# Layer 1 of a convolution–attention kernel: normalising in the channel layout with means and factors spread through DRAM, weight sums issued one by one, bias split moved

## The chip, the cores and the metric

The kernel runs on one core of a Trainium2 chip. A core has TensorE (matrix products), VectorE, ScalarE, GpSimd and SyncE, each with its own in-order queue; SyncE's queue issues the DMAs here. The metric is the device time of one launch in microseconds (us). Before the change it is 3277.91 us, the median of three runs (3275.79 to 3279.31).

## The reference, cut to what matters

The input is 8 images of 256 channels by 32x32 positions. Layer 0 (convolutions and attention) is not touched. Layer 1 takes each image as t, 1024 tokens of 256 channels:

```
def _ln_t(v, eps=1e-5):
    m = jnp.mean(v, axis=-1, keepdims=True)
    s = jnp.var(v, axis=-1, keepdims=True)
    return (v - m) / jnp.sqrt(s + eps)

t = t + _L1_attn_ref(_ln_t(t), WQ, WK, WV)        # causal attention, one head of 256
t = t + _L1_ffn_ref(_ln_t(t), Wr, br, W1, ...)    # 8 experts, three products each, gated by a softmax
```

The gate uses the mean of the second norm over the 8 images; each expert's last product adds a bias bo, weighted by the gate.

## The kernel before, in words

Layer 0 comes first, then layer 1's attention image by image, then the experts. All of t lies with channels on the 128 rows (two groups, KC = 2) and tokens along the row; the mean over channels is therefore a sum across rows.

`layer_norm` (L1351) does a norm in token layout. For each pair of 128-token tiles TensorE transposes t into PSUM (tile tpt, four transposes), ScalarE copies that to zt, and VectorE takes mean and variance of each token (`bn_stats`, `bn_aggr`, into mv). GpSimd makes the factor r from the variance in six small steps. Then VectorE scales zt in place (`scaled`, one 128x256 operation per tile), TensorE transposes it back (tile tpz, four transposes a pair), and ScalarE copies the result to the destination. It is used for the first norm (z of image b+1), for the second norm (z2 of image b-1, written to z_d), and in a half form for the last image (`second_norm_half`, L1440).

`causal(b)` (L1458) is the main stream of attention of image b: per 128-token tile i the scores s (TensorE, `scores`), their maximum nm (VectorE), the exponential (ScalarE), `norm` (masking, sum and reciprocal on VectorE, scaling on GpSimd), two to three tiles later `turn` (transposes tp, copies pT), and per 256 tokens `product` (po), which is added to t. The last quarter of image b-1 is done while image b runs.

`beside(b)` (L1532) is the side stream: first norm of b+1, a wait (`until`) for the last product of b-1, second norm of b-1, then `keys_values(b + 1)` (products pk and pv; the scores of b+1 need kk, z). `together` (L411) weaves both by hand: each generator yields its estimated us, and the side may run while its sum is under 0.85 times the main's. What is left of the side is issued after the main stream of that image is over. The engines keep this order. DMAs are placed by the scheduler into SyncE's queue.

There are three buffers for t. After the second norm of b, `second_norm` writes z_d and u_d (z2 and t) and loads t of b+3 into the freed buffer (L1432 to L1434). GpSimd adds z2 to feat. From image 2 on `weight_sums` (L1248) advances by one expert matrix per score tile: four VectorE operations of 128x128 at once and a DMA to sums_d.

At the start of the experts, from L1586: boT is made from the bias bo (split into two parts of low precision, transposed), in a pool hp that reuses the attention's memory; then `fetch(0)`, `fetch(1)`, the loads of the last half norm, and the 18 loads of sums_d are queued. Expert 0's first product pa needs none of them, expert 1's needs its sums ws.

Of the kernel before, what the change touches and what calls it, by code (L numbers as in the profile page):

```python
# [9 lines left out]
F32 = mybir.dt.float32  # L10
# [63 lines left out]
def conv_attn_hybrid_kernel(  # L74
# [1173 lines left out]
    def weight_sums(space):  # L1248


        for e in range(NE):
            for l in (0, 1, 2) if seven(e) else (0, 2):
                w_ = w_of[e][l]
                if e == 0:
                    s_ = sums_of[e][l] = wm.tile([P, 3, P], F32, tag=f"ws{e}_{l}", name=f"ws{e}_{l}")
                else:
                    s_ = space.tile([P, 3, P], F32, tag="ws", name="ws", bufs=2)
                a11, a21, a12, a22 = (w_[:, k, g * P : (g + 1) * P] for k in range(KC) for g in range(KC))
                dve.tensor_add(s_[:, 0, :], a21, a22)
                dve.tensor_sub(s_[:, 1, :], s_[:, 0, :], a11)  # L1260
                dve.tensor_sub(a21, a11, a21)
                dve.tensor_sub(s_[:, 2, :], a12, s_[:, 1, :])
                if e:
                    nc.sync.dma_start(sums_d[e, l], s_)
                yield
# [47 lines left out]
    with ExitStack() as l1:  # L1313
# [37 lines left out]
        def layer_norm(b, dst, tiles=range(NT)):  # L1351


            t0, n = tiles[0], len(tiles)
            zt = two.tile([P, NT, C], F32, tag="zt", name="zt", bufs=1)
            mv = tiny.tile([P, NT, 2], F32, tag="mv", name="mv", bufs=2)
            for i0 in range(0, n, 2):
                tp = ps_t.tile([P, 2, C], F32, tag="tp", name="tpt")
                for i in range(2):
                    for k in range(KC):  # L1360
                        c0 = (t0 + i0 + i) * P
                        pe.transpose(tp[:, i, k * P : (k + 1) * P], t[b][:, k, c0 : c0 + P], ident)
# [17 lines left out]
            for _ in range(4):  # L1380
# [6 lines left out]
            scaled(0)  # L1387
            yield 0.5
            for i0 in range(0, n, 2):
                if i0 + 2 < n:  # L1390
                    scaled(i0 + 2)
# [5 lines left out]
                yield 0.9  # L1397

        def first_norm(b):
            z[b] = two.tile([P, KC, N], F32, tag="z", name="z1")  # L1400
            yield from layer_norm(b, z[b])

        def keys_values(b):
            kk = kk_of[b] = two.tile([P, KC, N], F32, tag="kk", name="kk")
            for h in range(2):
                hs = slice(h * HALF, (h + 1) * HALF)
                for g in range(KC):
                    pk = ps_m.tile([P, HALF], F32, tag="mm", name="pk")
                    for k in range(KC):
                        pe.matmul(pk, at[:, k, g * P : (g + 1) * P], z[b][:, k, hs], start=(k == 0), stop=(k == KC - 1))  # L1410
                    act.copy(kk[:, g, hs], pk)
                    yield 1.7
            v = v_of[b] = two.tile([P, NT, C], F32, tag="v", name="v")
# [10 lines left out]
            while what not in done:  # L1424
                yield 0.7

        def second_norm(b):
            yield from until((b, N // QC - 1))
            z2 = two.tile([P, KC, N], F32, tag="z2", name="z2", bufs=1)
            yield from layer_norm(b, z2)  # L1430
            nc.sync.dma_start(z_d[b], z2)
            nc.sync.dma_start(u_d[b], t[b])  # L1432
            if b + 3 < B:
                load_t(b + 3)  # L1434
            if b == 0:
                pool.tensor_copy(feat, z2)
            else:
                pool.tensor_add(feat, feat, z2)
# [19 lines left out]
        def causal(b):  # L1458
            for i in range(NT):
                yield from scores(b, i)  # L1460
                yield from follow()
                if b >= 2:
                    next(sums, None)

        def follow():
# [10 lines left out]
        def scores(b, i):  # L1476
            q0, width = i * P, (i + 1) * P
            s = ps_s.tile([P, N], F32, tag="s", name="s1")
            for h in range(2):
                hs = slice(h * HALF, (h + 1) * HALF)  # L1480
                for k in range(KC):
                    pe.matmul(s[:, hs], z[b][:, k, q0:width], kk_of[b][:, k, hs], start=(k == 0), stop=(k == KC - 1))
                yield 1.7

            nm = tiny.tile([P, 1], F32, tag="nm", name="nm1")
# [44 lines left out]
            done.add((b, qc))  # L1530

        def beside(b):  # L1532
            if b + 1 < B:
                yield from first_norm(b + 1)
            if b >= 1:
                yield from second_norm(b - 1)
            if b + 1 < B:
                yield from keys_values(b + 1)
            else:
                yield from second_norm_half(b)  # L1540
                yield from gate(
                    0, feat, ps_m.tile([P, NT // 2, NE], F32, tag="mm", name="lg"), lambda: ps_t.tile([4 * NE, HALF], F32, tag="tp", name="pwT")
                )
# [8 lines left out]
        sums = weight_sums(two)  # L1552
        for _ in first_norm(0):
            pass
        for _ in keys_values(0):
            pass
        load_t(2)
        for b in range(B):

            if b == 2:  # L1560
                z0 = wm.tile([P, KC, HALF], F32, name="z0")
                nc.sync.dma_start(z0, z_d[0][:, :, :HALF])
            if b == 4:
                tz0 = column_sums(z0, wm.tile([P, 4, QC], F32, tag="tz0", name="tz0"))
            together(last() if b == B - 1 else causal(b), beside(b), 0.85)
        nc.sync.dma_start(u_d[B - 1][:, :, HALF:], t[B - 1][:, :, HALF:])
# [14 lines left out]
    with ExitStack() as l2:  # L1581
# [10 lines left out]
        bo_g = cols("bo").rearrange("p (e g) -> p g e", g=KC).unsqueeze(2).to_broadcast([P, KC, 2, NE])  # L1592
        bo4 = hp.tile([P, KC, 4, NE], F32R, name="bo4", bufs=1)
        dve.tensor_copy(bo4[:, :, 0:2, :], bo_g)
        dve.tensor_sub(bo4[:, :, 2:4, :], bo_g, bo4[:, :, 0:2, :].bitcast(F32))
        pb = ps_b.tile([4 * NE, KC, P], F32, tag="pm", name="pbo")
        for g in range(KC):
            pe.transpose(pb[:, g, :], bo4[:, g].bitcast(F32).rearrange("p a e -> p (a e)"), ident)
        dve.tensor_copy(boT, pb)
# [206 lines left out]
        zs[halves[0]] = z0  # L1806
        fetch(0)
        fetch(1)
        between = last_norm()
        next(between)  # L1810
        tz[halves[0]] = tz0
        for e in range(1, NE):
            for l in (0, 1, 2) if seven(e) else (0, 2):
                sums_of[e][l] = hp.tile([P, 3, P], F32, tag=f"ws{e}_{l}", name=f"ws{e}_{l}", bufs=1)
                nc.sync.dma_start(sums_of[e][l], sums_d[e, l])
        LAG2, LAG3 = 2, 4
        for n in range(len(pieces) + LAG3):
            one_ = two_ = three = iter(())
# [144 lines left out]
```

## Time and profile before

One execution was profiled; it took 3277.43 us, of which 3275.3 us are the span from its first to its last instruction.

| What | Before |
|---|---|
| median of the runs | 3277.91 us |
| profiled execution, and its span | 3277.43 us, 3275.3 us |
| TensorE busy | 3047.3 us, 93% |
| VectorE busy | 2417.4 us, 74% |
| ScalarE busy | 1438.2 us, 44% |
| GpSimd busy | 327.9 us, 10% |
| attention of layer 1, first scores to first expert product | 1439.63 to 2041.49 us |
| image 0 / 1 / 2 / 3 | 56.2 / 75.4 / 77.6 / 77.4 us |
| image 4 / 5 / 6 / 7 | 75.8 / 76.1 / 74.4 / 89.0 us |

Times inside the profile are us from the start of the span. A row of a timeline is: start, duration, engine, line, operation, output<-input, matrix or tile shape, count, and in brackets the idle time before it with what ended it. A matrix product of 32-bit numbers appears as two TensorE records. Nearly all rows carry L68, the line of the helper that keeps the program's order, so rows are told apart by tile names. The duration of a merged TensorE row includes the tail of its last product; the distance between starts is what TensorE is taken up.

### The profile page before, as it was taken

The numbers are of one execution on the slowest core, as the hardware profiler recorded it, in microseconds if no ns is written. First come the engines' busy times: TensorE is split into PE (matmuls) and PEld (weight loads), VectorE is DVE, ScalarE is ACT, GpSimd is POOL, SyncE is SP. The second block draws the span as 40 slices with busy tenths as digits, with TensorE's granted clock in tenths as the row PEclk, the third lists the DMA queues.
The fourth block names the chain that finished last, engine by engine and source line by source line (L and its number), as shares of the span: only waits on it lengthen the run. The fifth ranks groups of instructions, "written<-read, shape, count | busy, mean of one in ns | idle before, by whom it ended". The sixth has DMA issues, their size and how long they took to land.

```text
span 3275.3 us, 43158 instructions
## 1 busy us (share of the span) xinstructions
PE 3047.3 (93%) x17218; PEld 2050.7 (63%) x17218; DVE 2417.4 (74%) x3796; ACT 1438.2 (44%) x2227; POOL 327.9 (10%) x472
## 2 busy tenths in 40 slices
PE   7997999999999997779999998899999999999999
PEld 4554555555555554346556665678787777787787
DVE  5388888888888886735555444688888878888887
ACT  4554555555555553223333322444444444444443
POOL 2110212111111100011222111000000000000000
PEclk9998999999999999889999999999999999999999
DMA  3202020202020200031111101200000100000000
GB/s 111 53 1 52 27 52 27 53 27 52 27 52 27 52 14 20 4 136 44 50 61 51 39 26 72 75 20 20 20 20 20 33 20 20 20 20 26 20 7 13
DMA packets 49831, 121.45 MB, mean 37 GB/s; under 512 B 7302, under 2 KB 20054, under 8 KB 45782
## 3 DMA queue, kind: packets, MB, share of 16 engines
q1 hardware_dynamic: 49622, 118.61, 11.6%
q8 instruction: 137, 2.24, 0.3%
q14 instruction: 72, 0.59, 0.1%
HBM read 48.20 MB, written 37.88 MB: 26 GB/s over the span
## 4 chain that ended last, share of the span: by engine, by line
PE 48%; DVE 6%; ACT 1%; issue 1%; POOL 1%; DMA 0%; SPq 0%; ACTq 0%; POOLq 0%; DVEq 0%
PE pm L68 13%; PE pa L68 12%; PE q L68 12%; PE s L68 4%; PE po L68 3%; PE pv L68 2%; PE pk L68 2%; DVE nm L68 1%; DVE pr L68 1%; DVE zt L68 1%; DVE st L68 1%; ACT pr L68 1%; PE tp L68 1%; PE tpz L68 1%; PE tpt L68 1%
## 5 line engine op out<-in xcount | busy, mean ns | idle before, releaser
L68 ACT ACTIVATE h<-h,bn_o,bn_s 128x512 f32<-128x512 f32 x384 | 308.7, 813 | 627.7 <-DVE h L68 627.6
L68 DVE SCALAR_TENSOR_TENSOR x<-hpad,vec,x 128x1024 f32<-128x1024 f32 x248 | 320.4, 1297 | 32.1 <-ACT x L68 25.9
L68 DVE SCALAR_TENSOR_TENSOR conv<-hpad,vec,conv 128x1024 f32<-128x1024 f32 x256 | 331.5, 1301 | 14.3 <-ACT conv L68 8.4
L68 PE MATMUL pm<-h,w 128*128 128x512 f32 (+1 forms) x768 | 321.5, 528 | 0.0
L68 ACT ACTIVATE pT<-s 128x1024 f32<-128x1024 f32 x256 | 261.5, 1024 | 128.1 <-PE s L68 127.0
L68 PE MATMUL po<-pT,vT 128*32 128x256 f32 x4096 | 276.7, 388 | 12.0 <-ACT pT L68 11.3
L68 PE MATMUL ph<-xn,piw 128*128 128x512 f32 x512 | 250.8, 615 | 22.7 <-ACT conv L68 14.2
L68 PE MATMUL s<-kk,z 128*128 128x512 f32 x512 | 242.0, 600 | 0.6 <-DVE pr L68 0.6
L68 PE MATMUL s<-qst,kst 128*128 128x256 f32 x1024 | 216.5, 334 | 0.0
L68 PEld LDWEIGHTS s<-qst,kst 128*128 128x128 f32 x1024 | 146.5, 191 | 88.5 <-issue 82.2
L68 PEld LDWEIGHTS pm<-h,w 128*128 128x128 f32 x768 | 146.9, 191 | 76.6 <-issue 62.6
L68 DVE TENSOR_TENSOR h<-pa,first 128x512 f32<-128x512 f32 x128 | 88.3, 689 | 136.0 <-PE pa L68 134.3
L68 ACT ACTIVATE hpad<-ph,pi_o 128x512 f32<-128x512 f32 x126 | 87.0, 690 | 228.5 <-PE ph L68 228.4
L68 DVE TENSOR_TENSOR h<-h,wb 128x1024 f32<-128x1024 f32 x128 | 156.2, 1221 | 41.0 <-ACT h L68 41.0
L68 DVE SCALAR_TENSOR_TENSOR o<-vpad,pe_w,o 128x1024 f32<-128x1024 f32 x128 | 163.6, 1283 | 17.4 <-ACT o L68 14.7
L68 DVE TENSOR_TENSOR h<-h,first 128x256 f32<-128x256 f32 x384 | 163.2, 425 | 13.2
L68 PEld LDWEIGHTS ph<-xn,piw 128*128 128x128 f32 x512 | 88.9, 190 | 132.1 <-issue 89.1
L68 PE MATMUL pz<-pow__117,hid 128*128 128x256 f32 x512 | 129.2, 408 | 44.4 <-DVE hid L68 44.4
L68 PEld LDWEIGHTS po<-pT,vT 128*32 128x32 f32 x4096 | 107.5, 109 | 97.1 <-ACT pT L68 15.2
L68 PE MATMUL sums<-pT,ones 128*32 128x256 f32 x2048 | 158.7, 382 | 0.0
L68 PE MATMUL pa<-tz,ws 128*128 128x256 f32 x512 | 155.0, 385 | 3.8 <-DMA ws<-sums_d 3.8
L68 PE MATMUL q<-t,ws 128*128 128x256 f32 x512 | 152.8, 380 | 0.8 <-DVE t L68 0.8
(279 smaller groups left out, 5870.6 us busy)
## 6 DMA issues: line engine op xcount, KB each, us to landing
td<-t SPq DMA_DIRECT2D x8, 1024.0 KB, 3.8
t<-td SPq DMA_DIRECT2D x8, 1024.0 KB, 4.8
te<-ud SPq DMA_DIRECT2D x16, 512.0 KB, 4.0
out_dram<-te SPq DMA_DIRECT2D x16, 512.0 KB, 2.8
ze<-zd SPq DMA_DIRECT2D x15, 512.0 KB, 3.9
t<-in_x_dram SPq DMA_DIRECT2D x7, 1024.0 KB, 6.3
qst<-hi SPq DMA_DIRECT2D x56, 128.0 KB, 2.3
qst<-lo SPq DMA_DIRECT2D x56, 128.0 KB, 2.3
```

The costliest lines, as they stand in the source:

```text
L68: return self._tc.keep_in_program_order(method(*args, **kwargs))
```

## The change

The first norm of images 1 to 7 and the second norm of images 0 to 6 no longer go through zt and back. `statistics` transposes t and takes mean and variance as before (with the destination as scratch), GpSimd makes r and copies the means beside it, TensorE transposes this 128x16 tile (tpr), ScalarE copies it (rmT), and a DMA writes 16 rows of 128 numbers, 8 KB, to DRAM. `to_all_rows` reads them back with one DMA into rb, the same 8 KB on each of the 128 rows (1 MB, in the one buffer that zt has). `apply` computes (t - mean) * factor in t's own layout, eight VectorE operations of 128x512. `first_norm(0)` and the half norm keep `layer_norm`, whose pauses and look-ahead are changed.

The side stream is reordered: statistics(b+1), the wait, statistics(b-1), apply(b+1), keys, apply(b-1) with its DMAs, values. The load of t of b+3 stays in the step after the second norm, now `normed`, and so follows apply. Weight sums yield after every VectorE operation, start at image 1 and advance twice a tile. boT is made at the start of image 4. The queue at the start of the experts begins with the sums of expert 1.

```diff
+        def statistics(b, dst):
+            zt = dst.rearrange("p k n -> p (k n)").rearrange("p (i c) -> p i c", c=C)
...
+            pool.tensor_mul(r, r, y)
+            pool.tensor_copy(rm[:, 1, :], mv[:, :, 0])
+            for _ in range(4):
+                yield 1.0
+            tp = ps_t.tile([2 * NT, P], F32, tag="tp", name="tpr")
+            pe.transpose(tp, rm.rearrange("p a i -> p (a i)"), ident)
+            rmT = tiny.tile([2 * NT, P], F32, tag="rmT", name="rmT", bufs=1)
+            act.copy(rmT, tp)
+            rm_d[b] = dram.tile([2 * NT, P], F32, tag=f"rm{len(rm_d)}", name="rm_d")
+            nc.sync.dma_start(rm_d[b], rmT)
+            yield 0.2
+        def to_all_rows(b):
+            rb = rb_of[b] = two.tile([P, 2, N], F32, tag="zt", name="rb", bufs=1)
+            nc.sync.dma_start(rb.rearrange("p a n -> p (a n)"), rm_d.pop(b).rearrange("a n -> (a n)").partition_broadcast(P))
+        def apply(b, dst):
+            rb = rb_of.pop(b)
+            for h in range(2):
+                hs = slice(h * HALF, (h + 1) * HALF)
+                for k in range(KC):
+                    dve.tensor_sub(dst[:, k, hs], t[b][:, k, hs], rb[:, 1, hs])
+                    yield 0.6
+                    dve.tensor_mul(dst[:, k, hs], dst[:, k, hs], rb[:, 0, hs])
+                    yield 0.6
...
-        def second_norm(b):
-            yield from until((b, N // QC - 1))
-            z2 = two.tile([P, KC, N], F32, tag="z2", name="z2", bufs=1)
-            yield from layer_norm(b, z2)
+        def normed(b, z2):
             nc.sync.dma_start(z_d[b], z2)
             nc.sync.dma_start(u_d[b], t[b])
             if b + 3 < B:
...
         def beside(b):
-            if b + 1 < B:
-                yield from first_norm(b + 1)
+            more = b + 1 < B
+            if more:
+                z[b + 1] = two.tile([P, KC, N], F32, tag="z", name="z1")
+                yield from statistics(b + 1, z[b + 1])
+                to_all_rows(b + 1)
             if b >= 1:
-                yield from second_norm(b - 1)
-            if b + 1 < B:
-                yield from keys_values(b + 1)
+                yield from until((b - 1, N // QC - 1))
+                z2 = two.tile([P, KC, N], F32, tag="z2", name="z2", bufs=1)
+                yield from statistics(b - 1, z2)
+            else:
+                yield from pause(8)
+            if more:
+                yield from apply(b + 1, z[b + 1])
+            if b >= 1:
+                to_all_rows(b - 1)
+            if more:
+                yield from keys(b + 1)
+            else:
+                yield from pause(8)
+            if b >= 1:
+                yield from apply(b - 1, z2)
+                normed(b - 1, z2)
+            if more:
+                yield from values(b + 1)
             else:
                 yield from second_norm_half(b)
...
-        boT = hp.tile([4 * NE, KC, P], F32R, name="boT", bufs=1)
...
+                boT = wm.tile([4 * NE, KC, P], F32R, name="boT")
...
         zs[halves[0]] = z0
-        fetch(0)
-        fetch(1)
+        fetch_sums(1)
         between = last_norm()
         next(between)
+        fetch_sums(2)
+        fetch(0)
+        for e in range(3, NE):
+            fetch_sums(e)
+        fetch(1)
         tz[halves[0]] = tz0
```

More of the change, by code (lines that the diff above doesn't have):

```diff
@@ L1259, in weight_sums @@
                 dve.tensor_add(s_[:, 0, :], a21, a22)
+                yield
                 dve.tensor_sub(s_[:, 1, :], s_[:, 0, :], a11)
+                yield
                 dve.tensor_sub(a21, a11, a21)
+                yield
                 dve.tensor_sub(s_[:, 2, :], a12, s_[:, 1, :])
@@ L1378, in layer_norm @@
             pool.tensor_mul(r, r, y)
-            for _ in range(4):
+            for _ in range(6):
                 yield 1.0
@@ L1387, in layer_norm @@
             scaled(0)
+            if n > 2:
+                scaled(2)
             yield 0.5
             for i0 in range(0, n, 2):
-                if i0 + 2 < n:
-                    scaled(i0 + 2)
+                if i0 + 4 < n:
+                    scaled(i0 + 4)
                 tp = ps_t.tile([P, KC, 2, P], F32, tag="tp", name="tpz")
@@ L1397, in layer_norm @@
                 yield 0.9
+        rm_d, rb_of = {}, {}
+        def statistics(b, dst):
+            zt = dst.rearrange("p k n -> p (k n)").rearrange("p (i c) -> p i c", c=C)
+            mv = tiny.tile([P, NT, 2], F32, tag="mv", name="mv", bufs=2)
+            for i0 in range(0, NT, 2):
+                tp = ps_t.tile([P, 2, C], F32, tag="tp", name="tpt")
+                for i in range(2):
+                    for k in range(KC):
+                        c0 = (i0 + i) * P
+                        pe.transpose(tp[:, i, k * P : (k + 1) * P], t[b][:, k, c0 : c0 + P], ident)
+                act.copy(zt[:, i0 : i0 + 2, :], tp)
+                yield 0.6
+                for i in range(i0, i0 + 2):
+                    st = tiny.tile([P, 6], F32, tag="st", name="st")
+                    dve.bn_stats(st, zt[:, i, :])
+                    dve.bn_aggr(mv[:, i, :], st)
+                yield 0.6
+            y = tiny.tile([P, NT], F32, tag="y1", name="y1", bufs=2)
+            rm = tiny.tile([P, 2, NT], F32, tag="rm", name="rm", bufs=2)
+            r = rm[:, 0, :]
+            pool.tensor_scalar(y, mv[:, :, 1], LN_EPS, None, ALU.add)
+            pool.tensor_tensor(r, y, mhalf1, ALU.pow)
+            pool.tensor_mul(y, y, r)
+            pool.tensor_mul(y, y, r)
+            pool.tensor_scalar(y, y, -0.5, 1.5, ALU.mult, ALU.add)
+            pool.tensor_mul(r, r, y)
[9 more added lines that the diff above has]
+            yield 0.2
@@ new lines, in to_all_rows @@
+        def to_all_rows(b):
[5 more added lines that the diff above has]
+                hs = slice(h * HALF, (h + 1) * HALF)
+                for k in range(KC):
+                    dve.tensor_sub(dst[:, k, hs], t[b][:, k, hs], rb[:, 1, hs])
+                    yield 0.6
+                    dve.tensor_mul(dst[:, k, hs], dst[:, k, hs], rb[:, 0, hs])
+                    yield 0.6
@@ L1399, in first_norm, with pause @@
+        def pause(n):
+            for _ in range(n):
+                yield 1.0
         def first_norm(b):
@@ L1401, in first_norm, with keys @@
             yield from layer_norm(b, z[b])
-        def keys_values(b):
+        def keys(b):
             kk = kk_of[b] = two.tile([P, KC, N], F32, tag="kk", name="kk")
@@ L1412, in keys_values, with values @@
                     yield 1.7
+        def values(b):
             v = v_of[b] = two.tile([P, NT, C], F32, tag="v", name="v")
@@ L1461, in causal @@
                 yield from follow()
-                if b >= 2:
+                if b >= 1:
                     next(sums, None)
@@ L1482, in scores @@
                     pe.matmul(s[:, hs], z[b][:, k, q0:width], kk_of[b][:, k, hs], start=(k == 0), stop=(k == KC - 1))
+                if h == 0 and b >= 1:
+                    next(sums, None)
                 yield 1.7
@@ L1532, in beside @@
         def beside(b):
-            if b + 1 < B:
-                yield from first_norm(b + 1)
-            if b >= 1:
-                yield from second_norm(b - 1)
-            if b + 1 < B:
-                yield from keys_values(b + 1)
+            more = b + 1 < B
[3 more added lines that the diff above has]
+                to_all_rows(b + 1)
+            if b >= 1:
+                yield from until((b - 1, N // QC - 1))
[11 more added lines that the diff above has]
+                yield from pause(8)
+            if b >= 1:
+                yield from apply(b - 1, z2)
+                normed(b - 1, z2)
+            if more:
+                yield from values(b + 1)
             else:
@@ L1554, in conv_attn_hybrid_kernel @@
             pass
-        for _ in keys_values(0):
-            pass
+        for steps in (keys(0), values(0)):
+            for _ in steps:
+                pass
         load_t(2)
@@ L1563, in conv_attn_hybrid_kernel @@
             if b == 4:
+                boT = wm.tile([4 * NE, KC, P], F32R, name="boT")
+                bo_g = cols("bo").rearrange("p (e g) -> p g e", g=KC).unsqueeze(2).to_broadcast([P, KC, 2, NE])
+                bo4 = wm.tile([P, KC, 4, NE], F32R, name="bo4")
+                dve.tensor_copy(bo4[:, :, 0:2, :], bo_g)
+                dve.tensor_sub(bo4[:, :, 2:4, :], bo_g, bo4[:, :, 0:2, :].bitcast(F32))
+                pb = ps_m.tile([4 * NE, KC, P], F32, tag="mm", name="pbo")
+                for g in range(KC):
+                    pe.transpose(pb[:, g, :], bo4[:, g].bitcast(F32).rearrange("p a e -> p (a e)"), ident)
+                dve.tensor_copy(boT, pb)
                 tz0 = column_sums(z0, wm.tile([P, 4, QC], F32, tag="tz0", name="tz0"))
@@ L1587, in conv_attn_hybrid_kernel @@
         s2, o2 = bn_fold("g2", "be2", "m2", "v2", eps_moe, "bn2", extra="b2")
-        boT = hp.tile([4 * NE, KC, P], F32R, name="boT", bufs=1)
[L1592 to L1599, printed above, removed]
         def sums_tile(name):
@@ L1804, in last_norm, with fetch_sums @@
             )
-        zs[halves[0]] = z0
-        fetch(0)
-        fetch(1)
[L1809 to L1812, printed above, removed]
+        def fetch_sums(e):
             for l in (0, 1, 2) if seven(e) else (0, 2):
@@ L1815, in conv_attn_hybrid_kernel @@
                 nc.sync.dma_start(sums_of[e][l], sums_d[e, l])
+        zs[halves[0]] = z0
+        fetch_sums(1)
+        between = last_norm()
+        next(between)
+        fetch_sums(2)
[3 more added lines that the diff above has]
+        fetch(1)
+        tz[halves[0]] = tz0
         LAG2, LAG3 = 2, 4
```

## The prediction, on record before the run

> **What bounds the kernel now.** I read the page's busy times first, then a table of busy time by image, then the TensorE timeline of image 4 (an undisturbed one), with VectorE, GpSimd and the DMA queue beside it, and last the handover to the experts. The page says that TensorE sets the time:
>
> ```profile
> PE 3047.3 (93%) x17218; PEld 2050.7 (63%) x17218; DVE 2417.4 (74%) x3796; ACT 1438.2 (44%) x2227; POOL 327.9 (10%) x472
> ```
>
> So the change is worth what it takes off TensorE's own queue in the attention stage. By image (stretch: length, TensorE, weight loads, VectorE, ScalarE, GpSimd, clock, DMA):
>
> ```profile
> 1726.26:1802.05 75.79, 69.83 (x294) 45.44 (x293) 42.45 (x119) 24.20 (x44) 16.30 (x21) 1.00 0.14 55
> 1952.52:2041.49 88.97, 76.46 (x329) 53.84 (x329) 39.74 (x101) 20.15 (x38) 15.31 (x21) 0.94 0.12 48
> ```
>
> TensorE is idle 6 us of image 4. The groups of the stretch 1548 to 2000 show where:
>
> ```profile
> L68 PE MATMUL tpz<-ident,zt 128*128 128x128 f32 x176 | 30.9, 295 | 29.6 <-DVE zt L68 28.2 <-ACT z L68 1.4
> ```
>
> Nearly all idle time stands ahead of the transposes back (tpz), which the change removes. The TensorE timeline of image 4:
>
> ```profile
> 1716.98 1.88 PE L68 MATMUL s<-kk,z 128*128 128x512 f32 x4
> 1718.69 1.89 PE L68 MATMUL pv<-wv,z 128*128 128x256 f32 x8
> 1721.07 5.35 PE L68 MATMUL pv<-wv,z 128*128 128x256 f32 x24
> 1726.26 1.88 PE L68 MATMUL s<-kk,z 128*128 128x512 f32 x4
> 1727.97 1.04 PE L68 MATMUL tpt<-ident,t 128*128 128x128 f32 x8
> ...
> 1736.97 1.88 PE L68 MATMUL s<-kk,z 128*128 128x512 f32 x4
> 1739.92 0.67 PE L68 MATMUL tpz<-ident,zt 128*128 128x128 f32 x4 [1.07 <-DVE zt L68]
> ...
> 1766.11 3.60 PE L68 MATMUL s<-kk,z 128*128 128x512 f32 x8
> 1771.38 0.41 PE L68 MATMUL tpz<-ident,zt 128*128 128x128 f32 x2 [1.67 <-DVE zt L68]
> ...
> 1777.62 0.41 PE L68 MATMUL tpz<-ident,zt 128*128 128x128 f32 x2 [1.54 <-DVE zt L68]
> ```
>
> The reader is to see the period (scores of the image's last tile, values pv, next image's first scores at 1726.26, its transposes tpt at 1727.97) and the stalls. Beside it VectorE, GpSimd and the DMA queue:
>
> ```profile
> 1718.89 1.22 DVE L68 TENSOR_REDUCE nm<-s 128x1 f32<-128x1024 f32 x1 [3.36 <-PE s L68]
> 1724.04 0.17 DVE L68 RECIPROCAL rs<-rs 128x1 f32<-128x1 f32 x1
> 1725.88 0.68 DVE L68 TENSOR_TENSOR tz<-z 128x512 f32<-128x512 f32 x1
> 1739.07 0.20 POOL L68 TENSOR_TENSOR r<-r,y 128x8 f32<-128x8 f32 x1
> 1762.95 0.32 SPq L1324 DMA_DIRECT2D t<-td  x1
> ```
>
> The load of t is issued at 1762.95, right after the second norm's last tpt, and is needed at the next image's tpt near 1804: 41 us of slack for a transfer that lands in
>
> ```profile
> t<-td SPq DMA_DIRECT2D x8, 1024.0 KB, 4.8
> ```
>
> **What the Trainium skill says.** "TensorE: Matmul & The Clock Gate", What's actually happening: after an idle window of 3413 ns the array runs at half clock, until a busy window. The trace agrees: eight transposes take 1.94 us after 3.15 us of idleness, against 1.04 above.
>
> ```profile
> 1617.68 1.94 PE L68 MATMUL tpz<-ident,zt 128*128 128x128 f32 x8 [3.15 <-DVE zt L68]
> ```
>
> "SBUF — State Buffer", Who interferes with whom: a VectorE operation with two SBUF inputs contends with a GpSimd operation that reads SBUF. The trace agrees: w<-w takes 1.12 us at 1724.64 beside GpSimd's scaling, 0.29 at 1660.88 without. All eight operations of apply are of this kind. "DMA: Bandwidth & Descriptors", Rules for kernel authors: all 16 engines serve a DMA whose outermost dimension is a multiple of 16; the spread of rb has 128. No run here shows such a spread, and no page prices 128 reads of one row.
>
> **Part by part.** I cut image 4's period at Q = 1727.97 (tpt), E = 1755.52 (end of the last quarter's product) and T = 1794.49 (end of the last scores): Q to E 27.55, E to T 38.97, T to the next Q 9.3 us.
>
> Removed: 32 transposes at 0.11 us (eight take 0.87 start to start) are 3.5 us. Around them start-to-start gaps lose 1.2, 0.4, 0.8 (first norm) and 1.8, 0.5, 0.5, 1.7, 0.6 (second), 7.5 in all. Together 11 us an image.
>
> Added, by the order of the changed kernel's instructions on each engine:
>
> First tpr, between the two halves of tile 1's scores. GpSimd's r ends at 1739.27, 11.3 after Q; its copy of the means adds 0.25 (the y rows of the same shape). TensorE is there 10.7 after Q. Wait 0.9, transpose 0.2. Q to E becomes 27.55 - 4.3 + 1.1 = 24.35.
>
> Second tpr, inside tile 5's scores. Three of its four tpt groups now stand after tile 3's first half. VectorE does two groups of statistics (1.06 each), tile 3's maximum and norm (5.4 with ScalarE between), two weight sums, two groups; the last ends 12.7 after E, the GpSimd chain (3.43) at 16.3. TensorE is there at 12.8: wait 3.6. Behind it in TensorE's queue is everything else, tile 5's second half first.
>
> apply(b+1): eight operations at 0.68 (tz<-z row; 0.66 between starts). The first pk waits for the fourth of them, behind tile 5's maximum, norm and sums: ready 25.2 after E, TensorE there at 23.7, wait 1.5. The second pk waits for the addition of po to t, now behind the other four and tile 6's maximum: 1.2. E to T becomes 37.1.
>
> apply(b-1) and the load. After T, ScalarE's exponential waits for the last keys' copy (T+2.45), the norm ends at T+5.5, eight operations follow; the seventh, the last to read t, ends at T+10.9 (0.5 in it for GpSimd's scaling). Only then may t of b+2 be loaded into that buffer: 4.8 us, so Q comes at T+15.8. TensorE, after pk 1.7, turn 0.7, pv 6.9 and first scores 1.7, stands there at T+11.0. This is a new wait of 4.8 us with no work behind it that could pass: the queue is in order. It takes place at the starts of images 2 to 6. boT's transposes at image 4 wait for the same VectorE queue and end inside this wait: nothing.
>
> Period: 24.35 + 37.1 + 15.8 = 77.25, against 75.8; without the load's wait 72.45.
>
> Clock: an idle 4.8 us leaves most of one window empty wherever it lies; I take half clock after nine in ten, 1.7 us each: 7.7. After the second tpr, half as often and partly covered by the first pk's wait: 1.8.
>
> The spread: tpr to rb is a copy 0.5, a write (1.9, the row of 192 KB) and 4.8 (as 1 MB of t): 7.2. rb(b+1) has 29 us, rb(b-1), which waits for the buffer, 14.3 from issue to use: hidden up to there. SyncE's queue stands at rb's wait; the sums and the load behind it aren't due before.
>
> Weight sums: the same operations in other places, costed above. ScalarE loses eight copies an image: hidden.
>
> Last image: no load; 82.8 from first scores to the last po before. The tpz and their waits go (5), the half clocks of 2014 and 2024 go (5), and apply(6) ahead of the last maximum delays the last turn, so that po waits 5.0 instead of 2.3 and drops the clock twice (3.4): 73.3. Then the half norm's end and the gate are exposed (tpz 0.9, copies, feat, lg, softmax, pwT: 10.4, with a cold clock 11.7) where before
>
> ```profile
> 2041.11 0.58 PE L68 MATMUL pbo<-ident,bo 128*32 128x128 f32 x2 [5.19 <-DVE bo L68]
> 2050.43 0.81 PE L68 MATMUL pa<-tz,ws 128*128 128x256 f32 x2 [3.83 <-DMA ws<-sums_d]
> ```
>
> stood; both these waits go. From last po to expert 1's pa: 15.1 before, 16.9 after.
>
> Image 0 has no second norm: tpz and its waits less, 3.8.
>
> **Sum.** Image 0: -3.8. Images 1 to 6: 456.7 before (half clocks in it); 6 x 72.45 + 5 x 4.8 = 458.7, and 9.5 of clock: +11.5. Last image -9.5, handover +1.8. Together 0.0 on the profiled execution's 3277.43 us, which is 0.5 under the median: 3277.
>
> **Rivals.**
> - Even, as summed: 3277, 0.36, its own range 3270 to 3284.
> - The gain comes through: apply or the load is quicker than walked, or the short waits don't lower the clock. Without the 9.5 us of clock 3268; with t there in time as well (24 us less) 3244. For it speaks that 1 MB alone lands in 4.8; against, that no operation between T and the load can be left out. 0.33.
> - Slower: the load of t at the image's start is longer. Its neighbour is now z2's write of 1 MB, issued within a microsecond; the slowest of the eight loads took 7.7 us, among other traffic. 2.9 more, five times: 3291. It decides from 1.3 us a load (6.1 to land). The spread, if past 14.3 us, does the same. 0.31.
> - That the transposes aren't removed is excluded: the changed order has none but the half norms'.
>
> **Numbers.** A difference under 0.2% (6.5 us) can't be told from none here. Of the first case 0.30 lies within that and 0.03 on each side: faster 0.36, same 0.30, slower 0.34. The range, 3252 to 3295, leaves out the fullest gain and a slow spread, 0.2 together.
>
> **What would show it.** Right: tpt waiting some 5 us for t<-td at the starts of images 2 to 6, tpr waiting 1 and 4 us on GpSimd, pk on VectorE, no wait for ws. Wrong: tpt without a wait, images of 72 us (faster); or a wait for rb on VectorE (slower).

## The result and the profile after

The changed kernel takes 3282.80 us (median of 20 runs, 3278.78 to 3285.00) against 3279.43 us of the kernel before (20 runs, 3272.07 to 3282.12): ratio 1.0012, 95% interval 1.0005 to 1.0018. It is slower by 1.6 to 5.9 us, which is under the 0.2% bound of the prediction. The profiled execution took 3282.42 us with a span of 3280.7 us, 5.4 us more than the span before.

TensorE works less and yet the kernel isn't faster. The page's busy times:

```profile
PE 3034.5 (92%) x17008; PEld 2035.5 (62%) x17008; DVE 2455.5 (75%) x3796; ACT 1410.7 (43%) x2185; POOL 341.5 (10%) x486
```

Where the idle time of TensorE stands now, by the waits of TensorE from image 1 to the first experts (what waited, for whom, us in total, times, longest):

```profile
PE tpt L68 <- DMA t<-td: 30.0, 5, 6.8
PE tpr L68 <- POOL rm L68: 19.1, 13, 2.7
PE pk L68 <- DVE t L68: 7.6, 6, 2.1
PE po L68 <- ACT pT L68: 4.6, 1, 4.6
PE pbo L68 <- DVE bo L68: 2.8, 1, 2.8
```

In the kernel before, this view is led by

```profile
PE tpz L68 <- DVE zt L68: 32.0, 30, 3.1
```

The stalls ahead of the transposes back are gone, and in their place stand as many us of waiting for the load of t, plus 19 for the new transpose tpr. The TensorE timeline of image 4:

```profile
1726.52 0.38 PE L68 MATMUL pbo<-ident,bo 128*32 128x128 f32 x2 [2.81 <-DVE bo L68]
1726.74 1.88 PE L68 MATMUL s<-kk,z 128*128 128x512 f32 x4
1732.18 1.97 PE L68 MATMUL tpt<-ident,t 128*128 128x128 f32 x8 [3.57 <-DMA t<-td]
1733.95 2.65 PE L68 MATMUL s<-kk,z 128*128 128x512 f32 x4
...
1757.80 0.27 PE L68 MATMUL tp<-ident,pr 128*128 128x128 f32 x1
...
1773.50 0.38 PE L68 MATMUL tpr<-ident,rm 128*16 128x128 f32 x1 [2.71 <-POOL rm L68]
1773.67 3.26 PE L68 MATMUL s<-kk,z 128*128 128x512 f32 x4
...
1786.96 1.98 PE L68 MATMUL pk<-z,at 128*128 128x512 f32 x4 [1.40 <-DVE t L68]
...
1794.48 1.88 PE L68 MATMUL pk<-z,at 128*128 128x512 f32 x4
```

and the start of image 5 on TensorE, with SyncE's queue beside it:

```profile
1803.76 1.88 PE L68 MATMUL s<-kk,z 128*128 128x512 f32 x4
1812.42 1.97 PE L68 MATMUL tpt<-ident,t 128*128 128x128 f32 x8 [6.78 <-DMA t<-td]
1814.18 3.49 PE L68 MATMUL s<-kk,z 128*128 128x512 f32 x4
```

```profile
1805.61 0.32 SPq L1327 DMA_DIRECT2D t<-td  x1
1806.30 0.32 SPq L1496 DMA_DIRECT2D zd<-z  x1
```

The reader is to see three things. The load of t is issued at 1805.61, 11.1 us after the last scores (1794.48), because apply of the second norm must read the old t first. It lands 6.8 us later, and TensorE, which has reached tpt at 1805.64, waits for all of it. Behind the wait eight tpt take 1.76 us from start to start instead of 0.87, and four scores 3.3 instead of 1.7: the clock has been lowered. The list of DMA issues gives the median time from issue to landing of the transfers concerned (the five loads at the starts of images 2 to 6 are five of its eight; the three that the trace times take 6.67 to 6.76 us):

```profile
rb<-rm_d SPq DMA_DIRECT2D x14, 1024.0 KB, 4.7
t<-td SPq DMA_DIRECT2D x8, 1024.0 KB, 6.7
zd<-z SPq DMA_DIRECT2D x7, 1024.0 KB, 8.5
```

The difference of the two spans, cut at the same events (starts of scores, end of the last po of attention at 2035.33 before and 2035.21 after):

| Stretch | Before | After | Change | Predicted |
|---|---|---|---|---|
| up to the first scores | 1439.63 | 1438.61 | -1.0 | 0 |
| image 0 | 56.2 | 52.0 | -4.3 | -3.8 |
| images 1 to 6 | 456.7 | 473.0 | +16.3 | +11.5 |
| last image, to the end of the last po | 82.8 | 71.7 | -11.1 | -9.5 |
| from there to the end | 1240.0 | 1245.5 | +5.5 | +1.8 |
| sum | | | +5.4 | 0.0 |

The two rows from the last image on belong together: before, the half norm's tpz and the gate's products lg (2018.62 to 2026.44, 5.4 us of work) stand ahead of the last po, after they stand behind it. So some 5 of the 11.1 us are work that moved into the next row.

### The profile page after: what moved, and what is told of

Read it like the earlier page. It is cut to its first block, busy times and chain, and to the rows that moved or that the text cites. A ratio compares the mean times of both kernels' runs of the same rounds, so it can differ in the third digit from the quotient of the medians.

```text
span 3280.7 us, 42713 instructions
## 1 busy us (share of the span) xinstructions
PE 3034.5 (92%) x17008; PEld 2035.5 (62%) x17008; DVE 2455.5 (75%) x3796; ACT 1410.7 (43%) x2185; POOL 341.5 (10%) x486
## 4 chain that ended last, share of the span: by engine, by line
PE 46%; DVE 6%; ACT 1%; DMA 1%; POOL 1%; issue 1%; SPq 0%; POOLq 0%; ACTq 0%; DVEq 0%
PE pm L68 13%; PE pa L68 12%; PE q L68 12%; PE s L68 4%; PE po L68 2%; DVE z L68 2%; PE pk L68 1%; DMA t<-td 1%; DVE pr L68 1%; DVE nm L68 1%; PE tpt L68 1%; DVE st L68 1%; POOL rm L68 1%; ACT pr L68 1%; PE pv L68 1%
## 5 line engine op out<-in xcount | busy, mean ns | idle before, releaser
L68 DVE SCALAR_TENSOR_TENSOR x<-hpad,vec,x 128x1024 f32<-128x1024 f32 x248 | 320.4, 1297 | 32.1 <-ACT x L68 25.9
L68 PE MATMUL s<-kk,z 128*128 128x512 f32 x512 | 250.5, 621 | 0.6 <-DVE pr L68 0.6
L68 PEld LDWEIGHTS s<-qst,kst 128*128 128x128 f32 x1024 | 146.6, 191 | 89.0 <-issue 82.8
```

What stands on the lines that cost most here:

```text
L68: return self._tc.keep_in_program_order(method(*args, **kwargs))
```

## The experiments

The theory after the result: the kernel loses at the starts of images 2 to 6, where t is loaded too late; the load takes 6.7 instead of 4.8 us because the 1 MB write of z2 runs beside it; and the idleness lowers the clock. Rivals: the load hides another wait; the load is slow by itself; the products behind the wait are slow because of the DMA that has just landed and not because of the idleness; the loss lies in the handover, in the sums or in VectorE's queue. Each kernel was timed against the kernel before in rounds on the same chip.

**The four subtractions first** (e1_subs_first)

```diff
+            if not first:                      # second norm
+                for hs, k in parts:
+                    dve.tensor_sub(dst[:, k, hs], t[b][:, k, hs], rb[:, 1, hs])
...
+            for hs, k in parts:
+                if first:
+                    dve.tensor_sub(dst[:, k, hs], t[b][:, k, hs], rb[:, 1, hs])
...
+                dve.tensor_mul(dst[:, k, hs], dst[:, k, hs], rb[:, 0, hs])
...
```

> The changed kernel, with the four subtractions of the second norm's apply before its four multiplications, so that t is read for the last time three operations sooner. Theory (the waits of tpt for the load of t are what made the change a loss): the last subtraction ends some 2.0 us sooner (three operations of 0.69), so the five waits shrink from 6.7 to 4.7 us, 10 us in all: 3282.8 - 10 = 3273 us, and the clock still falls after each wait. If the write of z2, now 2.7 us behind the load instead of 0.7, also lets the load land in 4.8 us: waits of 2.8 us, 3263. Rival (the load only hides another wait, for VectorE's queue or ScalarE's copies, and tpt would wait for that instead): no change, 3282.

Measured: 3257.48 us, ratio 0.9931 (0.9917 to 0.9945), 25 us under the changed kernel. The total wait of tpt for the load falls from 30.0 to 11.9 us. The write of z2 follows the load by 2.4 us, and the three loads that the trace times land in 5.06, 5.83 and 4.91 us instead of 6.7. The rival falls: no other wait took the place (pk's for VectorE grew by 1.7 us in all). It is also more than the theory expected, since behind these waits of 2.80 to 3.28 us the clock stays up: the 10.7 us that it cost behind the loads fall to 0.9 in the profiled execution, which at 3251.62 us was the fastest of the five. Why it stays up is shown in the last section. TensorE at the start of image 5:

```profile
1791.32 1.09 PE L68 MATMUL tpt<-ident,t 128*128 128x128 f32 x8 [2.80 <-DMA t<-td]
1792.24 1.88 PE L68 MATMUL s<-kk,z 128*128 128x512 f32 x4
```

**The write of z2 later, first try** (e2_z_late)

```diff
+            if 0 < b < B - 2: held[b] = z2
+            else: nc.sync.dma_start(z_d[b], z2)
...
+                yield from statistics(b + 1, z[b + 1])
+                if b - 2 in held: nc.sync.dma_start(z_d[b - 2], held.pop(b - 2))
```

> The changed kernel, with the write of z2 of images 1 to 5 held back until after the next image's first statistics, so that the load of t has the DMA engines to itself. Theory (the load takes 6.7 us instead of the 4.8 of before because the 1 MB write of z2 is issued 0.7 us behind it): the load lands in 4.8 us, the waits of tpt are 4.8 instead of 6.7, five times 1.9: 3273 us. Rival (a load of 1 MB takes 6.7 us at this place with or without the write): waits of 6.7 as before, 3282.

Measured: 3283.36 us, ratio 1.0009 (1.0001 to 1.0017), waits of 29.9 us. It looks like the rival's number and says nothing: the scheduler put the write back where it had been, as SyncE's queue shows.

```profile
1807.12 0.32 SPq L1327 DMA_DIRECT2D t<-td  x1
1807.81 0.32 SPq L1608 DMA_DIRECT2D zd<-z  x1
```

**The write of z2 later, from ScalarE's queue** (e2c_z_late)

```diff
                 act.copy(zt[:, i0 : i0 + 2, :], tp)
+                if i0 == 2:
+                    for h in list(held):       # z2 of images 1 to 4
+                        act.dma_start(z_d[h], held.pop(h))
...
+            if 0 < b < B - 3:
+                held[b] = z2
...
```

> The changed kernel, with the writes of z2 of images 1 to 4 issued from ScalarE's queue, behind its second copy of the next image's first statistics, so that they start after the load of t has landed (in the earlier try the scheduler put them 0.7 us behind the load again). Four of the five loads then have the DMA engines to themselves. Theory (the write of 1 MB, issued 0.7 us behind the load, stretches it): the four loads land in 4.8 us, their waits shrink from 6.7 to 4.8, 7.6 us in all: 3275 us. Rival (a load takes 6.7 us at this place with or without the write, for instance because it starts at the end of a chain through semaphores): waits of 6.7 stay, 3283.

Measured: 3275.42 us, ratio 0.9988 (0.9982 to 0.9995), 7.4 us under the changed kernel where 7.6 were expected. At images 3 to 6 the write now starts after the load has landed, and the wait is the load alone. Image 5, with the queues of SyncE and ScalarE:

```profile
1804.42 0.32 SPq L1327 DMA_DIRECT2D t<-td  x1
1809.28 1.97 PE L68 MATMUL tpt<-ident,t 128*128 128x128 f32 x8 [4.85 <-DMA t<-td]
1811.37 0.33 ACTq L68 DMA_DIRECT2D zd<-z  x1
```

The waits at images 3, 5 and 6 are 4.84, 4.85 and 5.03 us. The load at image 2, whose neighbour is the write of z2 of image 0, kept it, and a wait of 6.67. So the 1.9 us between 4.8 and 6.7 are the price of the neighbour. Image 4 is less clean: its load took 5.72 us alone, for a reason that was not found.

**The wait filled with products** (e5_filled, e5c_filled). The products are extra work, whose result nobody reads.

```diff
+                if i0 == 0 and b >= 3 and dst is z.get(b):
+                    fill = ps_t.tile([P, HALF], F32, tag="tp", name="fill")
+                    for n in range(12):        # e5c: 6, with at as both operands
+                        pe.matmul(fill, at[:, 0, :P], feat[:, 0, :HALF], start=True, stop=True)
```

> The changed kernel, with 12 extra products of 128x512 (two records each, 0.43 us for a record by the s rows, 0.86 a product: 10.3 us if all are so; their result is read by nobody) queued on TensorE ahead of the first tpt of images 2 to 6, that is in the load's wait. Theory (the wait also lowers the clock, and eight tpt at 1.97 instead of 1.04 us with the scores behind them at 3.62 instead of 1.88 cost some 2.3 us each time): the extra products replace 6.7 us of waiting by 10.3 us of work, +3.6 less 2.3 = +1.3 us five times, 3289 us, with tpt at 1.04. Rival (the slow records are not the clock after idleness but reads disturbed by the DMA that has just landed): tpt stays at 1.97, 3282.8 + 5 x 3.6 = 3301 us.

Measured: 3320.85 us, ratio 1.0127 (1.0111 to 1.0142), more than either side expected. The edit itself was at fault: the products read feat, which GpSimd was just adding to, and waited 19.2 us for it. The records of tpt behind them took 1.04 us, which is against the rival, but the time can't be used. So a second try, half as many products on an operand that is never written:

> The changed kernel, with 6 extra products of 128x512 (12 records at 0.43 us: 5.2 us; their operand is never written in the loop, their result is read by nobody) on TensorE ahead of the first tpt of images 2 to 6, in the load's wait. Theory (the wait also lowers the clock: in the changed kernel the eight tpt take 1.76 from start to start instead of 0.87, the four scores 3.41 instead of 1.72, the next tpt 0.82 instead of 0.43, 3.0 us together): the products cost nothing, being shorter than four of the waits and 1.6 us longer than that of image 4, the records behind them are at full speed, 5 x 3.0 - 1.6 = 13 us less: 3269 us. Rival (they are slow because of the DMA that has just landed): tpt stays at 1.97, 3284 us.

Measured: 3275.00 us, ratio 0.9986 (0.9979 to 0.9992), 7.8 us less for 26 us more of work. Start of image 5:

```profile
1801.57 5.31 PE L68 MATMUL fill<-at 128*128 128x512 f32 x12
1808.65 1.09 PE L68 MATMUL tpt<-ident,t 128*128 128x128 f32 x8 [1.77 <-DMA t<-td]
1809.58 1.88 PE L68 MATMUL s<-kk,z 128*128 128x512 f32 x4
```

The DMA has just landed here too, and the transposes and scores behind it run at full speed: the rival falls, it is the idleness. The size is smaller than expected because I took 3.0 us for each wait from one image; from the first tpt to the next, the changed kernel loses 2.5, 2.6, 1.7, 2.5 and 1.4 us against 2.59 undisturbed, 10.7 in all. Filling and the rests of the waits come to 32.0 us instead of 30.0, so 8 to 9 us should remain; 7.8 did. "TensorE: Matmul & The Clock Gate" in the Trainium skill (What's actually happening) states that the array goes to half clock after an idle window of about 3.4 us; the runs agree that idleness lowers the clock, but waits of 2.71 us ahead of tpr can lower it too, so a whole idle window is not needed here, and the measurement decides (last section).

**Apply early, subtractions first** (e6_both). Besides the edit of e1:

```diff
-                yield from keys(b + 1)
+                yield from keys(b + 1, (0,))
             if b >= 1:
-                yield from apply(b - 1, z2)
+                yield from apply(b - 1, z2, first=False)
                 normed(b - 1, z2)
             if more:
+                yield from keys(b + 1, (1,))
                 yield from values(b + 1)
```

> The changed kernel, with the four subtractions first and apply of the second norm moved between the two halves of keys, so that they stand on VectorE ahead of the last tile's maximum. Theory (the waits for the load are the loss): the load is issued some 11 us sooner and lands before TensorE is at tpt; the waits of 30.0 us in all and about 2.3 us of clock behind each go, 41 us: 3242 us, less what VectorE's later maximum of tile 7 gives back (4 x 0.69 = 2.8 us on a chain that nothing on TensorE waits for before the first scores of the next image). Rival (the loss lies in VectorE's longer queue): the maximum and the norm of the last tile, 3 us later, hold up the next image's turns, and of the 41 us at least half stays: 3262 us or more.

Measured: 3236.40 us, ratio 0.9870 (0.9855 to 0.9885), 46 us under the changed kernel and 43 under the kernel before. At the start of image 5 the load has landed before TensorE is there:

```profile
1779.80 1.04 PE L68 MATMUL tpt<-ident,t 128*128 128x128 f32 x8
```

The wait for the load is gone from the view of TensorE's waits, which is now led by

```profile
PE tpr L68 <- POOL rm L68: 19.1, 13, 2.7
PE pk L68 <- DVE t L68: 12.1, 6, 2.2
```

From the first scores of image 1 to those of the last image the profiled execution takes 428.0 us, the changed kernel 473.0, and this account closes: 30.0 us of waits, pbo's 2.8, 10.7 of clock behind the loads and 7.9 of clock behind tpr go; 4.5 of waiting for VectorE and 1.6 of clock behind one such wait (image 2) come: 45.3 for 44.9. Another 2.8 us lie in the experts. That the clock behind tpr recovers too had not been expected: tpr waits 2.7 us as before, but from it to the first pk the changed kernel needs 8.7 to 8.9 us in images 2 to 6, this one 7.2 to 7.4. This part comes from where the waits lie in time and not from the earlier load as such (last section).

**The handover undone, and alone** (e7_no_handover_b, e8_handover_only_b)

```diff
 if b == 4:
-    boT = wm.tile([4 * NE, KC, P], F32R, name="boT")
...
+boT = hp.tile([4 * NE, KC, P], F32R, name="boT", bufs=1)
...
-fetch_sums(1)
+fetch(0)
+fetch(1)
 between = last_norm()
 next(between)
-fetch_sums(2)
-fetch(0)
-for e in range(3, NE):
+for e in range(1, NE):
     fetch_sums(e)
-fetch(1)
```

> The changed kernel, with boT and the order of the loads at the start of the experts as before. Theory (the handover's part is a gain of its own): the waits of pbo (5.2 us) and of pa for ws (3.8 us) come back at the start of the experts; at image 4 pbo's 2.8 us goes, but the load's wait behind it grows by as much: 3282.8 + 9.0 = 3292 us. Rival (the prediction's: these waits stand beside the gate's exposed steps, so that only a part of them shows): 3285 us or less.

> The kernel before, with only the handover's part of the change: boT at the start of image 4, sums of expert 1 first. Theory: both waits at the start of the experts go, 9.0 us, and at image 4 pbo waits at most 2.8 us for VectorE: 3279.5 - 9.0 + 2.8 = 3273 us. Rival (behind the waits the loads of the last half norm become late, which stood behind them in SyncE's queue): 3279 us or more.

Measured: without it the changed kernel takes 3284.19 us, ratio 1.0013 (1.0006 to 1.0019), 1.4 us more, which the intervals don't tell from none; alone on the kernel before it gives 3270.24 us, ratio 0.9971 (0.9963 to 0.9980), 9 us less. So the same edit is worth its two waits where these stand alone, and nearly nothing where the gate is exposed: the changed kernel's last gate ends after the last po, and the preparation of boT and the loads of the sums lie beside it. With the handover undone, pbo follows pwT after 1.35 us in which nothing is waited for; the 5.19 of before are not there.

```profile
2048.89 1.01 PE L68 MATMUL pwT<-ident,g 128*32 128x128 f32 x4 [2.01 <-DVE g L68]
2051.25 0.59 PE L68 MATMUL pbo<-ident,bo 128*32 128x128 f32 x2 [1.35 <-issue]
```

The profiled execution of e8 was at the upper end of its runs (3277.69, of 3265.42 to 3277.69), with a clock of 0.86 in its first 100 us of experts against 0.94 before; it shows the first expert product 5.0 us sooner (2036.48 for 2041.49) and the wait for ws gone, and the rest of the 9 us rests on the medians.

**Weight sums as before** (e4_sums_block)

```diff
                 dve.tensor_add(s_[:, 0, :], a21, a22)
-                yield
                 dve.tensor_sub(s_[:, 1, :], s_[:, 0, :], a11)
-                yield
...
-                if b >= 1:
+                if b >= 2:
                     next(sums, None)
```

> The changed kernel, with the weight sums as before: four operations at once, one matrix for each score tile, from image 2 on. Theory (the prediction's: the same operations in other places cost nothing by themselves, since no wait of TensorE ends on one of them): 3283 us, within 3. Rival (they stand ahead of apply on VectorE at the end of an image, where the chain to the load of t runs: four at once are 1.0 us instead of 0.5 there, so each of the five load waits grows by 0.5 us, and the second tpr's wait by as much): 3288 us.

Measured: 3285.18 us, ratio 1.0020 (1.0013 to 1.0026). The difference from the changed kernel, 2.4 us, lies between the two expectations, nearer to the prediction's; the intervals overlap. The second tpr of image 4 waits 3.64 instead of 2.71 us there, as the rival said, while the load's wait behind it is 0.4 us shorter (6.37 for 6.78):

```profile
1776.54 0.28 PE L68 MATMUL tpr<-ident,rm 128*16 128x128 f32 x1 [3.64 <-POOL rm L68]
```

Splitting the sums is worth some 2 us, and it may be nothing.

**The other waits** (e9_tuned, e10_tuned). On e6, six operations of the first norm's apply move ahead of the second tpr:

```diff
-            for _ in range(4):
+            for _ in range(pauses):            # 6 for the second norm
+                next(beside_, None)            # apply(b + 1)
                 yield 1.0
...
                 yield from keys(b + 1, (0,))
+                if b >= 1:
+                    yield from pause(2)        # e10 only
```

> The kernel with the early load (four subtractions first, apply of the second norm between the halves of keys), and besides with six operations of apply of the first norm moved ahead of the second tpr, which itself is put two steps later. Theory (the waits left in it are tpr's 2.7 us for GpSimd's chain and pk's 2.2 us for the addition to t, both for want of work between): tpr's falls to some 0.4, pk's to some 1, 3.5 us in each of six images: 3236 - 21 = 3215 us. Rival (the spread is no longer hidden: rb of the second norm is asked for only after tpr and lands some 7 us later, by 1.3 for the write and 4.6 for the spread, while its apply now stands about 4 us behind tpr on VectorE; VectorE then waits 3 us ahead of the addition to t, and pk behind it): 3236 us or more.

> As the run before it in this call (early load, six operations of the first norm's apply ahead of a later tpr), with two more steps between the first half of keys and apply of the second norm, so that on VectorE it stands behind the norm of tile 6, where rb has landed by the estimate of 7 us behind tpr. Theory: tpr's wait falls from 2.7 to some 0.4 us, pk's from 2.2 to under 1, no wait for rb: 3236 - 21 = 3215 us. Rival (VectorE, not the order, is the limit of this stretch, and the waits move to tile 6's or 7's turns): 3230 us or more.

Measured: e9 3275.66 us, ratio 0.9987 (0.9980 to 0.9993): 39 us are lost again, by the rival's mechanism and more than its size. VectorE waits for the spread:

```profile
1704.23 1.29 DVE L68 TENSOR_TENSOR z<-t,rb 128x512 f32<-128x512 f32 x2 [3.65 <-DMA rb<-rm_d]
```

Behind it all of apply stands ahead of the maximum of tile 7 (1712.50), ScalarE's exponential waits for that maximum (10.99 us), its copies of kk wait behind the exponential, and TensorE waits for them:

```profile
1716.21 10.06 PE L68 MATMUL pv<-wv,z 128*128 128x256 f32 x32 [7.07 <-ACT kk L68]
```

With two steps more between (e10) the spread has landed: 3227.25 us, ratio 0.9843 (0.9829 to 0.9856), the fastest here, 52 us under the kernel before. The waits of tpr for GpSimd fall from 19.1 to 2.6 us, and those of pk for VectorE (12.1 in e6) are gone; others, six of up to 1.9 us for VectorE and six of up to 1.6 for ScalarE's kk, took part of their place, so it is 9 us faster than e6 and not 21.

```profile
PE s L68 <- DVE pr L68: 10.8, 6, 1.9
PE pv L68 <- ACT kk L68: 9.5, 6, 1.6
PE tpr L68 <- POOL rm L68: 2.6, 6, 0.5
```

## Why the prediction was right and wrong

The mechanism on record was right: the waits that it names are there, except that of the first pk, and none of size in the images that it doesn't name. The loads of t at images 2 to 6 became the new bound and ate the gain. The forecast of no difference was wrong: the kernel became slower by little, but by more than the noise, +3.4 us by the medians where 0.0 had been summed. By the steps of image 4 (the clock's price shared out; Q, E and T as in the prediction):

| Step | Predicted | Measured |
|---|---|---|
| Q to E, with 1.5 of clock | 25.9 | 25.6 |
| first tpr's wait | 0.9 | 0.45 |
| E to T, with 0.4 of clock | 37.5 | 36.7 |
| second tpr's wait | 3.6 | 2.71 |
| first pk's wait, second pk's | 1.5, 1.2 | 0, 1.40 |
| T to the issue of the load | 10.9 | 11.1 |
| landing of the load | 4.8 | 6.8 |
| T to the next Q | 15.8 | 17.9 |

- **The step that failed is the size of one term: "Only then may t of b+2 be loaded into that buffer: 4.8 us".** The duration came from a row of the kernel before, where the load ran without the write of z2 beside it (there the load is issued at 1762.95 and the write at 1779.53). I had the neighbour as the slow rival ("z2's write of 1 MB, issued within a microsecond") and gave it 2.9 us and a chance of 0.31; it is 1.9 us: the load took 6.7 to 6.8. Five waits came to 30.0 us, and pbo's 2.8 ahead of one of them, where 24 had been put. This term is enough to turn the sign: with four of the five neighbours moved away (e2c) the kernel takes 3275.42 us, ratio 0.9988 (0.9982 to 0.9995).
- **Clock.** Behind the loads 10.7 us against 7.7 predicted. Behind the second tpr 8.1 us in images 2 to 6 against 1.8: "half as often and partly covered" did not hold here, it came in all five, and the first pk's wait that should have covered part of it is not there. In e1 it came in four images, in e6 in none; what decides it is where the wait lies (last section). The prediction took "the trace agrees" from a wait of 3.15 us, which is shorter than the idle window of 3413 ns beside it.
- **What was overestimated.** The first pk doesn't wait (9.0 us had been put for six images), and both tpr wait less (18.5 us instead of 27.0). This returned 17.5 us, nearly all of the 18.1 that the load (8.8) and the clock (3.0 and 6.3) cost too much. That the whole sum missed by only 5 us is therefore luck.
- **Image 0** came out as said (-4.3 for -3.8). **The last image** came near it (-11.1 for -9.5), but its working doesn't carry the number: 82.8 less 5 and 5, plus 2.7 for po's longer wait and 3.4 of clock, is 78.9 and not 73.3. The half norm's tpz and the gate's lg, which leave this stretch for the next, are counted in the handover and not named here; their 5.4 us would nearly fill the gap. Po waited 4.64 us, close to the 5.0 said, and the clock fell once (1.8 us) and not twice.
- **Handover.** Right up to expert 1's first product: from the end of the last po it takes 16.6 us (2051.76 - 2035.21) against 16.9 predicted. The rest of the +5.5 us, 4.0, lies in the experts behind it, whose code is the same: the granted clock of the 30 us from 2035.30 on is 0.74 against 0.89 before. From expert 1's first product on, TensorE stands at half clock for 24.9 us against 18.6 before, which at half speed can cost 3.2 of the 4.0 us. It is not a fixed price of the change: from the same point e1 and e6 need 1226.1 us, the changed kernel 1228.9, the kernel before 1224.9. Why half clock comes more often there was not separated.
- **The spread** was hidden as estimated: no wait for rb in the changed kernel. e9 shows the point from which it is not.
- **The weight sums** cost nothing that can be told from the measurement (e4).

## What to carry to other kernels

When a step is put in place of another, look for the last reader of each buffer that a load will overwrite: here the products removed were worth their price, and the load behind the new last reader took it back, until the reads were put first and the step moved ahead (3236 instead of 3283 us). Price a transfer with what is issued beside it, not by its row in a quieter place. And count a wait of several us on TensorE with the slow products behind it, which here cost another 1.4 to 2.6 us each wherever more than 2 us of the wait fell into one window of the clock (next section).

## What the hardware showed that was not expected

- Loads of 1 MB landed in 4.7 to 4.9 us alone (before and e6; one in 5.72 in e2c), in 4.9 to 5.8 with a write of 1 MB issued 2.4 us behind (e1), in 6.7 to 6.8 with one 0.7 us behind; the write itself took 8.5 us there (median), and 3.8 in e6, where it follows the load by 7.7 us.
- The spread of one row of 8 KB to 128 rows landed in 4.7 us, as fast as 1 MB of distinct rows.
- The first multiplication of the second norm's apply took 1.49 us instead of 0.69 (0.8 more, where 0.5 had been put) at 1800.80 and again at 1881.88, while GpSimd scaled pr for 1.58 us from 1800.17 and from 1881.25.
- The four waits of e1 for the load, 2.80 to 3.28 us, left the clock up, one of 3.57 in the changed kernel didn't. But tpr's 2.71 us lowered it in five images of six of the changed kernel (2.30 us in the last of them), in four of e1 and in none of e6. The traces show what decides: in every profiled execution here the granted clock changes only on a fixed grid of 3.413 us, and what counts is how much idleness falls into one window of it. Two windows of the changed kernel, then two of e6, around the second tpr of image 2 (stretch: length, busy time of TensorE, weight loads, VectorE, ScalarE, GpSimd, granted clock, DMA); the wait is 2.72 us in both:

```profile
1609.19:1612.60 3.41, 0.69 (x3) 0.31 (x3) 2.69 (x8) 1.22 (x3) 2.62 (x6) 1.00 0.01 2
1612.60:1616.01 3.41, 3.41 (x7) 1.41 (x6) 3.01 (x7) 0.20 (x1) 1.40 (x1) 0.50 0.01 2
1599.64:1603.05 3.41, 1.48 (x4) 0.38 (x2) 2.69 (x7) 1.15 (x2) 2.31 (x4) 1.00 0.01 2
1603.05:1606.47 3.42, 2.63 (x10) 1.46 (x11) 3.31 (x9) 0.27 (x2) 1.96 (x5) 1.00 0.01 2
```

In the first case all 2.72 us of idleness fall into one window, and the next is at half clock; in the second they are split, 1.93 and 0.79, and the clock stays up. So it is in images 1 to 6 of the changed kernel and of the ten experiments built on it: each of the 75 windows at full clock in which TensorE was idle for 2.03 us or more was followed by one at half clock, and none of the 1290 with 1.99 or less (in the kernel before one with 1.95 was too). A longer wait can thus leave the clock up where it lies across two windows, as in e1, and that e6 keeps the clock behind tpr comes from the place of the waits, which nobody planned.
